# A fixed convolution moved from VectorE to TensorE: one more chunk of channels as Toeplitz products

## The chip, the cores and the metric

The kernel runs on one core of one Trainium2 chip. A core has five engines that run their own instruction streams: TensorE (PE: matrix products into PSUM), VectorE (DVE), ScalarE (ACT), GpSimd (POOL) and SyncE (SP, which here only issues DMA). The metric is the device time of one execution in microseconds, the median over several runs.

## What is computed

A Perceiver-like network of four layers with 1024 tokens (16 batches of 64) of 256 features; each layer has a cross-attention, a mixer and a feed-forward part. All is float32. The change concerns the mixer of layer 1, a Mamba-like block with a fixed, not input-dependent, state space. Cut to what matters:

```python
xz = rmsnorm(x) * norm_w @ in_proj_w.T + in_proj_b
x_ssm, gate = split(xz, 2)                                # 512 channels each
xc = conv_general_dilated(x_ssm, conv_w, ...)             # dense over channels, 4 taps in time
x_ssm = silu(xc + conv_b)
A_bar = exp(sigmoid(dt) * A)
K = einsum('dn,dn,dnl->dl', C_param, B_bar, A_bar ** l_range)   # 64 taps for each channel
ssm = causal_depthwise_conv(x_ssm, K) + x_ssm * D_param   # "the fixed convolution"
out = (ssm * silu(gate)) @ out_proj_w.T + out_proj_b
```

The fixed convolution gives each of 512 channels its own causal filter of 64 taps over the 64 tokens of a batch.

## The kernel before

The twelve blocks of the network follow one another in one program (`BLOCKS`). The mixer is `mamba_conv`. Inside it, and inside the attention before it (`xattn_folded("L1_xattn")`), `set_order(True)` makes PE, DVE and ACT each run their instructions in the order in which the Python code issues them (`mm` and `tr`, L207 and L210, for PE; the `Queue` objects `dve` and `act`, L72, for the others). So almost all instructions of this stage carry the line of a helper: L208 products, L211 transposes, L72 all of DVE and ACT; the names of their tiles tell them apart. SP's and POOL's DMA queues are put in order by the scheduler, and run first in, first out.

The 512 channels lie in four chunks (c = 0 to 3) of 128 partitions, the 1024 tokens along the free axis in two halves (n = 0, 1) of 512.

- `project(i, n)` (L1236): two products of 512 columns into `psi`; i = 0 to 3 gives the input `xp` of chunk i (ACT adds the bias), i = 4 to 7 the gate `gs` of chunk i - 4 (ACT's silu). It is a generator that can be stopped after its first product.
- `convolved(c, n)` (L1261): the dense four-tap convolution, 16 products of 512 columns into `psc`, then ACT's silu into `xs`. A generator too, stopping after every four products.
- The fixed convolution is done in two ways. For chunks 0, 1 and 2 `taps` (L1278) lets DVE do the 64 taps, each a multiply and add of the shifted tokens by a per-channel scalar, into two accumulators (even and odd taps) that are summed at the end; `gated` (L1291) multiplies by the gate into `o`. For chunk 3 it is a Toeplitz product on PE: `tokens` (L1294) transposes `xs[3]` so that tokens lie on partitions (`xt`), `toeplitz(i, ...)` (L1303) takes 32 channels at a time; for each channel d it multiplies that channel's 64 x 64 Toeplitz matrix with the channel's tokens, twice (for partitions 0 to 63 and 64 to 127), 8 columns each (`psT`), and ACT copies the block into `yt`. At the end `pso` transposes it back and DVE gates it into `o`.
- `part(c, t)` (L1320): the output projection of chunk c for token tile t, one product of 256 columns accumulated in PSUM (`po`) over the chunks; `added` adds it to the residual `X`.

The Toeplitz matrices are made in the attention before: `conv_taps` (L1152) computes the filters and writes those of chunk 3, with zeros ahead, to DRAM (`d_K`, L1190); then `tap_rows(s)` (L1193), called four times at each of 16 steps of the attention's loop (L867 to L869), copies one shifted window of it, DRAM to DRAM, into row s of `d_T` (L1195), 32 KB. These 64 copies go out on SP's queue, among the attention's loads of `cT` (L657, L659) and `cx` (L666). In `toeplitz` SP loads the matrices of 32 channels into `T` (L1307), two DMAs of 512 KB, four buffers.

The order of the stage: projections and convolution of chunk 0, gate of chunk 0, DVE starts chunk 0's taps; PE goes on with the convolutions of chunks 1, 2 and 3, while DVE does the taps of 1 and 2; then `tokens`, and `toeplitz` with other work dealt into it: before every sixth channel (`every`) it takes one step of the generator `rest` (L1326), that is the gates 5, 6, 7, then `part` of chunk 0, the gating of chunk 1 on DVE, and `part` of chunk 1. What is left of `rest` follows, then `gated` and `part` of chunk 2, then the transposes, gating and `part` of chunk 3 with the residual sums.

## Time and profile before

| | |
|---|---|
| median of 3 runs | 3028.03 us (3027.95 to 3032.76) |
| the profiled execution | 3034.92 us, span 3033.2 us |
| PE / DVE / ACT / POOL busy | 95% / 64% / 44% / 24% |
| mean granted clock of PE | 0.965 |
| the mixer `mamba_conv`, from its first projection to its last `po` | 1153 to 1344 us |
| DVE's taps of chunks 0, 1, 2 | 1177.0 to 1316.1 us |
| row copies `d_T<-d_K` on SP | 64, from 895.2 to 944.1 us, 2.3 us from issue to landing |
| loads `T<-d_T` on SP | 8, issued 1177.0 to 1181.4 us, 6.9 us to landing |

The profile is one execution. Times on the left of a timeline's line count from the span's start; the bracket gives how long the engine was idle before the group and what ended that. PE counts as busy while any product is in flight, so a busy PE can still be a slow one: the column PEclk gives the share of its full clock that the chip's throttle granted. Each product of this float32 kernel stands in the profile as two records. The granted clock is 1.00 in most of the span, and 0.50 in stretches.

### The profile page before, as it was taken

The page shows a single profiled execution, that of the slowest core. Times are in us where ns is not written, and L with a number is a line of the kernel's source. Part 1 is how long each engine was busy: PE and PEld are TensorE (multiplying, and loading weights), DVE is VectorE, ACT ScalarE, POOL GpSimd, SP SyncE. Part 2 cuts the span into 40 slices and gives each one's busy share as a digit, 9 for nine tenths or more (in the row PEclk, how much of TensorE's full clock was granted, in tenths as well). Part 3 has the DMA queues.
Part 4 walks back from the last instruction along what each step waited for, and adds up shares of the span by engine and source line. Part 5 has one row for each costly group of instructions (what it writes and reads, how often), then busy time and mean ns, then how long its engine had stood idle before and what let it go on. Part 6 is the DMA issues. An engine that isn't in the chain of part 4 may idle for free.

```text
span 3033.2 us, 65778 instructions
## 1 busy us (share of the span) xinstructions
PE 2872.8 (95%) x27656; PEld 1824.3 (60%) x27656; DVE 1951.5 (64%) x4061; ACT 1322.6 (44%) x3049; POOL 737.7 (24%) x817
## 2 busy tenths in 40 slices
PE   8999999999999999987999999997999899998889
PEld 4666666666555554466875555546985454545677
DVE  6888886524776665952127777768975667775521
ACT  4555554412554441002335444448951255554222
POOL 1000002400210001014530100026961454542142
PEclk9999999999999999978999999998999999999889
DMA  2011000014223313026862222201111211110243
GB/s 75 23 44 33 23 30 13 18 35 113 65 82 96 102 47 85 21 70 244 294 237 64 75 75 80 61 22 39 57 54 40 67 59 63 66 46 15 73 141 124
DMA packets 75839, 225.26 MB, mean 74 GB/s; under 512 B 17431, under 2 KB 30586, under 8 KB 68632
## 3 DMA queue, kind: packets, MB, share of 16 engines
q1 hardware_dynamic: 47568, 115.57, 12.6%
q0 software_dynamic: 21728, 99.34, 9.7%
q10 hardware_dynamic: 6248, 6.14, 0.7%
q8 instruction: 219, 3.59, 0.5%
q14 instruction: 76, 0.62, 0.1%
HBM read 210.09 MB, written 14.49 MB: 74 GB/s over the span
## 4 chain that ended last, share of the span: by engine, by line
PE 80%; DVE 13%; ACT 2%; POOL 2%; issue 2%; DMA 1%; DVEq 0%; POOLq 0%; ACTq 0%; SPq 0%
PE pss L208 15%; PE o L208 14%; PE pu L208 8%; PE pd L208 7%; PE psp L208 6%; PE pkv L208 6%; PE pst L211 4%; PE po L208 2%; PE psq L208 2%; PE pb L208 2%; DVE h L72 1%; PE psy L208 1%; PE py L1655 1%; PE pg L208 1%; PE ptk L211 1%
## 5 line engine op out<-in xcount | busy, mean ns | idle before, releaser
L208 PE MATMUL pss<-cT,qw 128*32 128x256 f32 x8192 | 360.8, 381 | 5.7 <-ACT pr L72 5.7
L72 DVE TENSOR_REDUCE nm<-pss 128x2 f32<-128x512 f32 (+1 forms) x384 | 314.5, 861 | 68.6 <-PE pss L208 68.5
L208 PE MATMUL o<-pT,cx 128*64 128x512 f32 (+3 forms) x1088 | 351.7, 576 | 0.0
L72 ACT ACTIVATE pr<-pss,nmm 128x256 f32<-128x256 f32 x512 | 234.4, 484 | 151.1 <-DVE nmm L72 151.1
L208 PEld LDWEIGHTS pss<-cT,qw 128*32 128x32 f32 x8192 | 201.1, 108 | 133.0 <-issue 18.2
L225 POOL TENSOR_SCALAR rs<-mv 128x8 f32<-128x8 f32 (+3 forms) x50 | 10.0, 200 | 1084.1 <-DVE mv L243 609.6
L208 PEld LDWEIGHTS o<-pT,cx 128*64 128x64 f32 (+1 forms) x1088 | 134.3, 163 | 188.4 <-issue 167.1
L208 PE MATMUL pkv<-wx,cT 128*128 128x512 f32 (+1 forms) x512 | 193.4, 632 | 0.6 <-issue 0.6
L72 ACT ACTIVATE pr<-pr,sm 128x256 f32<-128x256 f32 x256 | 109.1, 497 | 192.5 <-DVE sm L72 192.5
L72 DVE TENSOR_SCALAR pr<-pr,sm 128x256 f32<-128x256 f32 (+1 forms) x384 | 169.6, 484 | 6.3
L211 PEld LDWEIGHTS pst<-ident,pr 128*128 128x128 f32 x1024 | 114.5, 141 | 69.1 <-DVE pr L72 25.0
L208 PE MATMUL pd<-wd,hT 128*128 128x256 f32 x656 | 151.6, 382 | 2.6 <-DVE hT L2903 1.4
L72 DVE STREAM_TRANSPOSE pT<-pr 128x1024 f32<-128x1024 f32 x128 | 151.8, 1224 | 2.2
L2661 DVE TENSOR_SCALAR y<-pd,row 128x256 f32<-128x256 f32 x39 | 18.9, 484 | 205.3 <-PE pd L208 205.3
L1648 POOL TENSOR_TENSOR h<-h,cb 128x1024 f32<-128x1024 f32 x63 | 147.2, 2390 | 11.5 <-DVE h L72 11.3
L72 DVE TENSOR_TENSOR_SCAN h<-dA,pb 128x512 f32<-128x512 f32 x128 | 145.3, 1200 | 4.8 <-PE pb L211 2.2
L72 ACT ACTIVATE pr<-pss,nm 128x1024 f32<-128x1024 f32 x128 | 141.9, 1117 | 3.0 <-DVE nm L72 3.0
L208 PEld LDWEIGHTS pd<-wd,hT 128*128 128x128 f32 x656 | 122.1, 190 | 30.3 <-DVE hT L2903 5.6
L211 PE MATMUL pst<-ident,pr 128*128 128x128 f32 x1024 | 136.0, 276 | 2.0 <-DVE pr L72 1.3
L208 PEld LDWEIGHTS pkv<-wx,cT 128*128 128x128 f32 (+1 forms) x512 | 64.5, 189 | 118.3 <-issue 92.2
L1881 POOL TENSOR_TENSOR rnk<-rnk,mhalf 128x8 f32<-128x8 f32 (+1 forms) x84 | 130.0, 1548 | 7.0
L72 ACT COPY pT<-pst 128x512 f32<-128x512 f32 x128 | 75.0, 586 | 127.5 <-PE pst L211 127.5
(567 smaller groups left out, 5820.4 us busy)
## 6 DMA issues: line engine op xcount, KB each, us to landing
cT<-in_ctxT SPq DMA_DIRECT2D x32, 768.0 KB, 4.3
cx<-in_ctxP SPq DMA_DIRECT2D x32, 768.0 KB, 4.2
cT<-in_ctxT SPq DMA_DIRECT2D x32, 512.0 KB, 3.9
cT<-in_ctxT SPq DMA_DIRECT2D x64, 256.0 KB, 4.9
offb<-d_off SPq DMA_DIRECT2D x16, 576.0 KB
cb<-d_C SPq DMA_DIRECT2D x16, 512.0 KB, 3.7
wu<-in_L_ffn_w POOLq DMA_DIRECT2D x8, 1024.0 KB, 5.5
wd<-in_L_ffn_w POOLq DMA_DIRECT2D x8, 1024.0 KB, 6.2
```

Of the source, the lines that this page charges most:

```text
L72: ins = getattr(self.engine, op)(*args, **kwargs)
L208: self.in_order(self.nc.tensor.matmul(out, lhsT=lhsT, rhs=rhs, start=start, stop=stop))
L211: self.in_order(self.nc.tensor.transpose(out, in_, self.ident))
L225: nc.gpsimd.tensor_scalar(t[:p, :n], in_, scale, eps, ALU.mult, ALU.add)
L1648: nc.gpsimd.tensor_tensor(hs[i], hs[i], cbs[hf, g], ALU.mult)
L1655: nc.tensor.matmul(py[:, t, ch], lhsT=x, rhs=self.ident, start=start, stop=stop, is_transpose=True, skip_group_check=True,)
L1881: nc.gpsimd.tensor_tensor(r, r, self.mhalf[:, : n * H], ALU.pow)
L2661: nc.vector.tensor_scalar(y[:, i, :], po[:, i * D : (i + 1) * D], weight[:, g + i : g + i + 1], None, ALU.mult)
```

## The change

The fixed convolution of chunk 2 goes the way of chunk 3, as Toeplitz products on PE; DVE keeps the taps of chunks 0 and 1. For this
- two sets of filters are written (`d_K[0]`, `d_K[1]`), and every `tap_rows` issues two copies, 128 in all;
- the order becomes: convolutions of chunks 1 and 3, taps of chunk 1, `tokens(3)`, `toeplitz(3)` with the convolution of chunk 2 dealt in (one step of four products before every 14th channel), `tokens(2)`, `toeplitz(2)` with `rest` dealt in (before every fifth channel);
- `rest` now has the gates 7, 5, 6; after gate 7 the transposes back and the gating of chunk 3 (`channels(3)`), after gate 5 the gating of chunk 1; then `part` of chunks 0, 1 and 3. `channels(2)` and `part` of chunk 2 end the stage;
- 16 loads of `T` instead of 8 through the same four buffers.

```diff
-        self.d_K = dram.tile([P, 2 * TQ - 1], F32, name="d_K")
-        self.d_T = dram.tile([TQ, P, TQ], F32, name="d_T")
+        self.d_K = [dram.tile([P, 2 * TQ - 1], F32, name=f"d_K{c}") for c in (2, 3)]
+        self.d_T = [dram.tile([TQ, P, TQ], F32, name=f"d_T{c}") for c in (2, 3)]
...
-        zk = pool.tile([P, 2 * TQ - 1], F32, name="tapz")
+        zk = pool.tile([P, 2, 2 * TQ - 1], F32, name="tapz")
         nc.gpsimd.memset(zk, 0.0)
-        nc.gpsimd.tensor_copy(zk[:, TQ - 1 :], self.taps[:, 3, :])
-        nc.sync.dma_start(out=self.d_K, in_=zk)
+        nc.gpsimd.tensor_copy(zk[:, :, TQ - 1 :], self.taps[:, 2:4, :])
+        for i in range(2):
+            nc.sync.dma_start(out=self.d_K[i], in_=zk[:, i])
...
-        self.nc.sync.dma_start(out=self.d_T[s], in_=self.d_K[:, TQ - 1 - s : 2 * TQ - 1 - s])
+        for i in range(2):
+            self.nc.sync.dma_start(out=self.d_T[i][s], in_=self.d_K[i][:, TQ - 1 - s : 2 * TQ - 1 - s])
...
-            def tokens(g):
+            def tokens(c):
...
-            def toeplitz(i, more, every):
+            def toeplitz(c, i, more, every):
                 T = two.tile([P, TB, TQ], F32, tag="T", name="T", bufs=4)
...
                 for d in range(TB):
                     if (i * TB + d) % every == 0:
                         next(more, None)
                     for r in (slice(0, 64), slice(64, 128)):
-                        self.mm(ps[r, d, :], T[r, d, :], xt[r, :, i * TB + d])
+                        self.mm(ps[r, d, :], T[r, d, :], xts[c][r, :, i * TB + d])
...
+            def channels(c):
+                for g in range(2):
+                    ps = mid.tile([P, 512], F32, tag="m", name="pso")
+                    for k in range(4):
+                        self.tr(ps[:, k * P : (k + 1) * P], yts[c][:, 4 * g + k, :])
+                    cols = slice(g * 512, (g + 1) * 512)
+                    dve.tensor_tensor(o[:, c, cols], ps, gs[:, c, cols], ALU.mult)
...
             def rest():
-                for i in (5, 6, 7):
+                for i in (7, 5, 6):
                     for h in range(2):
                         yield from project(i, h)
-                for t in range(0, NT, 2):
-                    part(0, t)
-                    part(0, t + 1)
-                    yield
-                gated(*sums[1])
-                for t in range(0, NT, 2):
-                    part(1, t)
-                    part(1, t + 1)
-                    yield
+                    if i == 7:
+                        channels(3)
+                    if i == 5:
+                        gated(*last_sum)
+                for c in (0, 1, 3):
+                    for t in range(0, NT, 2):
+                        part(c, t)
+                        part(c, t + 1)
+                        yield
...
-            for c in (1, 2, 3):
+            for c in (1, 3):
                 for n in range(2):
                     conv(c, n)
-                if c < 3:
-                    sums[c] = taps(c, 0, B)
-            for g in range(2):
-                tokens(g)
+            last_sum = taps(1, 0, B)
+            tokens(3)
+            more = (x for n in range(2) for x in convolved(2, n))
+            for i in range(P // TB):
+                toeplitz(3, i, more, 14)
+            for _ in more:
+                pass
+            tokens(2)
             more = rest()
             for i in range(P // TB):
-                toeplitz(i, more, 6)
+                toeplitz(2, i, more, 5)
             for _ in more:
                 pass
-            gated(*sums[2])
-            for t in range(NT):
-                part(2, t)
...
+            channels(2)
...
             for t in range(NT):
-                part(3, t)
+                part(2, t)
```

More of the change, by code (lines that the diff above doesn't have):

```diff
@@ L1228, in mamba_conv @@
             gs = one.tile([P, 4, N], F32, name="gs")
-            xt = one.tile([P, NT, P], F32, name="xt")
-            yt = one.tile([P, NT, P], F32, name="yt")
+            xts, yts = ({c: one.tile([P, NT, P], F32, name=f"{n}{c}") for c in (2, 3)} for n in ("xt", "yt"))
             o = one.tile([P, 4, N], F32, name="o")
@@ L1292, in gated @@
                 dve.tensor_tensor(o[:, c, cols], acc.rearrange("p b t -> p (b t)"), gs[:, c, cols], ALU.mult)
-            def tokens(g):
-                ps = mid.tile([P, 512], F32, tag="m", name="pst")
-                x = xs[3].rearrange("p b t -> p (b t)")
-                for k in range(4):
-                    t = 4 * g + k
-                    self.tr(ps[:, k * P : (k + 1) * P], x[:, t * P : (t + 1) * P])
-                act.copy(xt[:, 4 * g : 4 * g + 4, :], ps.rearrange("p (t d) -> p t d", t=4))
-            def toeplitz(i, more, every):
+            def tokens(c):
+                x = xs[c].rearrange("p b t -> p (b t)")
+                for g in range(2):
+                    ps = mid.tile([P, 512], F32, tag="m", name="pst")
+                    for k in range(4):
+                        t = 4 * g + k
+                        self.tr(ps[:, k * P : (k + 1) * P], x[:, t * P : (t + 1) * P])
+                    act.copy(xts[c][:, 4 * g : 4 * g + 4, :], ps.rearrange("p (t d) -> p t d", t=4))
+            def toeplitz(c, i, more, every):
                 T = two.tile([P, TB, TQ], F32, tag="T", name="T", bufs=4)
                 for r in range(2):
-                    ins = nc.sync.dma_start(out=T[64 * r : 64 * r + 64], in_=self.d_T[:, i * TB : (i + 1) * TB, :])
+                    ins = nc.sync.dma_start(
+                        out=T[64 * r : 64 * r + 64], in_=self.d_T[c - 2][:, i * TB : (i + 1) * TB, :]
+                    )
                     tc.add_manual_dep(ins.ins, started[0], sync, reason="behind the taps' weights")
@@ L1313, in toeplitz @@
                     for r in (slice(0, 64), slice(64, 128)):
-                        self.mm(ps[r, d, :], T[r, d, :], xt[r, :, i * TB + d])
-                act.copy(yt[:, :, i * TB : (i + 1) * TB], ps.rearrange("p d t -> p t d"))
+                        self.mm(ps[r, d, :], T[r, d, :], xts[c][r, :, i * TB + d])
+                act.copy(yts[c][:, :, i * TB : (i + 1) * TB], ps.rearrange("p d t -> p t d"))
+            def channels(c):
+                for g in range(2):
+                    ps = mid.tile([P, 512], F32, tag="m", name="pso")
+                    for k in range(4):
+                        self.tr(ps[:, k * P : (k + 1) * P], yts[c][:, 4 * g + k, :])
+                    cols = slice(g * 512, (g + 1) * 512)
+                    dve.tensor_tensor(o[:, c, cols], ps, gs[:, c, cols], ALU.mult)
             pos = [held.tile([P, 2, D], F32, tag="o", name="po") for _ in range(NT // 2)]
             def part(c, t):
-                first, last = t % 2 == 0 and c == 0, t % 2 == 1 and c == 3
+                first, last = t % 2 == 0 and c == 0, t % 2 == 1 and c == 2
                 self.mm(pos[t // 2][:, t % 2], o[:, c, t * P : (t + 1) * P], wo[:, c, :], first, last)
-            sums = {}
             def rest():
-                for i in (5, 6, 7):
+                for i in (7, 5, 6):
                     for h in range(2):
                         yield from project(i, h)
-                for t in range(0, NT, 2):
-                    part(0, t)
-                    part(0, t + 1)
-                    yield
-                gated(*sums[1])
-                for t in range(0, NT, 2):
-                    part(1, t)
-                    part(1, t + 1)
-                    yield
+                    if i == 7:
[7 more added lines that the diff above has]
+                        yield
             for c in range(4):
@@ L1349, in mamba_conv @@
                 gated(*x)
-            for c in (1, 2, 3):
+            for c in (1, 3):
                 for n in range(2):
                     conv(c, n)
-                if c < 3:
-                    sums[c] = taps(c, 0, B)
-            for g in range(2):
-                tokens(g)
+            last_sum = taps(1, 0, B)
[6 more added lines that the diff above has]
+            tokens(2)
             more = rest()
             for i in range(P // TB):
-                toeplitz(i, more, 6)
+                toeplitz(2, i, more, 5)
             for _ in more:
                 pass
-            gated(*sums[2])
-            for t in range(NT):
-                part(2, t)
-            for g in range(2):
-                ps = mid.tile([P, 512], F32, tag="m", name="pso")
-                for k in range(4):
-                    self.tr(ps[:, k * P : (k + 1) * P], yt[:, 4 * g + k, :])
-                cols = slice(g * 512, (g + 1) * 512)
-                dve.tensor_tensor(o[:, 3, cols], ps, gs[:, 3, cols], ALU.mult)
+            channels(2)
             def added(lo, hi):
```

## The prediction, made before the changed kernel ran

> **What bounds the kernel now.** I read the page first, then the chain of waits, then the timelines of PE, DVE and SP, and last the granted clock by stretches of 3.41 us.

> ```profile
> span 3033.2 us, 65778 instructions
> PE 2872.8 (95%) x27656; PEld 1824.3 (60%) x27656; DVE 1951.5 (64%) x4061; ACT 1322.6 (44%) x3049; POOL 737.7 (24%) x817
> ```

> PE is busy 95% of the span, so work added to it costs time unless it fills a hole. The profiled execution took 3034.92 us (span 3033.2); the median of the runs is 3028.03, 6.9 lower. Durations below are the profile's, and the difference is put on the median.

> The change lies between 1177 and 1345 us. From 1177.02 to 1317.4 the chain of waits runs over DVE's taps. Chunk 2's taps run from 1272.98 to 1316.13:

> ```profile
> 1272.98 0.75 DVE L72 TENSOR_SCALAR acc20e<-xs,taps 128x1024 f32<-128x1024 f32 x1
> ...
> 1317.27 1.22 DVE L72 TENSOR_TENSOR o<-acc20e,gs 128x1024 f32<-128x1024 f32 x1
> ```

> PE's timeline there (start, length, idle time before it in brackets):

> ```profile
> 1198.43 82.61 PE L208 MATMUL psc<-xp,wc 128*128 128x512 f32 x192
> ...
> 1301.80 0.87 PE L208 MATMUL psT<-xt,T 64*64 64x8 f32 x24
> 1302.60 1.12 PE L208 MATMUL psi<-xnT,w_in 128*128 128x512 f32 x2
> ...
> 1311.09 0.87 PE L208 MATMUL psT<-xt,T 64*64 64x8 f32 x24
> 1317.40 2.08 PE L208 MATMUL po<-wo,o 128*128 128x256 f32 x4 [5.44 <-DVE o L72]
> 1319.41 1.45 PE L208 MATMUL psT<-xt,T 64*64 64x8 f32 x24
> 1320.79 2.07 PE L208 MATMUL po<-wo,o 128*128 128x256 f32 x4
> ...
> 1329.57 3.16 PE L208 MATMUL psT<-xt,T 64*64 64x8 f32 x56
> 1332.66 6.08 PE L208 MATMUL po<-wo,o 128*128 128x256 f32 x16
> 1338.57 1.04 PE L211 MATMUL pso<-ident,yt 128*128 128x128 f32 x8
> 1340.02 3.72 PE L208 MATMUL po<-wo,o 128*128 128x256 f32 x16 [0.42 <-DVE o L72]
> ```

> PE works without a hole until 1311.96, waits 5.44 us for DVE, and is then slow: the same 24 small records take 1.45 us for 0.87, four `po` records 2.07 for 1.13. The granted clock says why (columns: stretch, its length, PE busy, PEld, DVE, ACT, POOL, PEclk, DMA, GB/s):

> ```profile
> 1306.74:1310.16 3.42, 3.42 (x57) 2.64 (x56) 3.42 (x9) 0.00 (x0) 0.00 (x0) 1.00 0.22 87
> 1310.16:1313.57 3.41, 1.80 (x28) 1.32 (x28) 3.41 (x12) 0.37 (x1) 0.00 (x0) 1.00 0.00 0
> 1313.57:1316.98 3.41, 0.00 (x0) 0.00 (x0) 3.38 (x10) 0.00 (x0) 0.00 (x0) 0.50 0.00 0
> ...
> 1323.81:1327.22 3.41, 3.41 (x34) 2.56 (x34) 0.00 (x0) 0.00 (x0) 0.00 (x0) 0.50 0.00 0
> ...
> 1334.05:1337.46 3.41, 3.41 (x9) 2.70 (x8) 0.00 (x0) 0.00 (x0) 0.00 (x0) 0.50 0.00 0
> 1337.46:1340.88 3.42, 3.00 (x18) 2.48 (x17) 1.29 (x2) 0.00 (x0) 0.00 (x0) 1.00 0.00 0
> ```

> **What PE gets, and what it saves.** A product shows as two records. Unit prices at full clock: 512 columns 0.4294 us (82.44/192, from 1198.43 to 1280.87), 256 columns half of it, a transpose 0.133 (1.04/8). Of 24 small records the starts span 0.87-0.20 = 0.67 us, 29 ns a record, 0.117 us for a channel's four. A round of 24 small and two wide records takes 1.85 us; less 0.70 and 0.86 this leaves 0.285 us for changing to small products and back.

> From 1198.43 the new order on PE is:
> - four half chunks of convolution (chunks 1 and 3), 128 x 0.4294 = 54.96: 1253.39;
> - tokens(3), as now from 1280.87 to 1282.31, 1.44: 1254.83;
> - toeplitz(3) with chunk 2's convolution dealt in: 64 x 0.4294 + 128 x 0.117 + 8 rounds x 0.285 = 27.48 + 14.95 + 2.28 = 44.71: 1299.54;
> - tokens(2), eight transposes and a handover, 1.2: 1300.7;
> - toeplitz(2): 14.95 + 24 rounds x 0.285 (6.84) + 24 `psi` records (10.31) + 48 `po` records (10.31) + eight transposes of channels(3) (1.06) = 43.47: 1344.2;
> - the last `yt` copy, today behind 16 `po`, now bare: 0.37 and two handovers, 0.7: 1344.9.

> There the closing transposes (`pso`) start, today at 1338.57: **+6.3 us**. Put otherwise, PE gets 21.3 us (14.95 small, 12 more rounds 3.4, 16 transposes and a handover 2.3, the bare copy 0.7) and gets back 15.0: the 5.44 us wait and some 9.5 us of half clock. For the order of now the same sum at full clock and without the wait ends at 1323.6; with both put in it ends at 1338.5, against 1338.57.

> Removed from DVE: chunk 2's 64 taps, their sum and gate, 44.3 us. It is worth only those 15.0, because PE comes next, directly. Added to DVE: two 128x512 gates (0.69 each, free since 1274). Added to ACT: two `xt` copies (0.58) and four `yt` copies (0.37), beside PE; ACT is 44% busy. Uncovered, these would cost 4 us.

> **SP's queue.** 64 more row copies (`tap_rows`, L1195) and eight more loads of T (0.6 us issue, landing 6.9). The first T of chunk 2 can issue when block 0 of chunk 3 is done (near 1267) and is used after 1301: hidden; uncovered it would cost 7 us. The queue behind them holds nothing until the next stage's write. The row copies stand among the attention's loads:

> ```profile
> 938.31 6.36 SPq L1195 DMA_DIRECT2D d_T<-d_K  x10
> 948.50 0.33 SPq L657 DMA_DIRECT2D cT<-in_ctxT  x1
> 978.90 3.66 PE L208 MATMUL pss<-cT,qw 128*32 128x256 f32 x64
> ```

> Up to 938.3 the queue has as many rows ahead of each load as now. Then 35 rows, a `cx`, 17 rows, and the cT now issued at 948.50. At 0.65 to 0.77 us a row (the groups x10 to x31) it issues at 972 to 979, lands 4.9 later, at 977 to 984, and scores start at 978.90: 0 to 5 us, I take 1.5 (0.70 a row). The `cx` behind 22 more rows lands near 997, used at 999.94: hidden. The two 127-column writes and doubled copy on POOL: nothing, the rows wait for the first write as now.

> **The clock.** The last wide product of chunk 2 goes in at channel 98. Then 30 channels (3.5 us of small products) and eight transposes run without one. To weigh this I counted, for every 3.41 us window, the share in which columns stream (0.84 ns a column and record: 0.4294/512; overlaps once). All 23 windows after which the clock fell have at most 0.42, the 798 after which it stayed at least 0.42; it rose after 24 of at least 0.82, and stayed half after 46, all but one at most 0.71. Small products alone stream 0.23, transposes 0.80, the dealt rounds 0.5 to 0.57: these neither lose the clock nor win it back. A window inside the small stretch loses it: 0.23 x 3.5 + 0.8 x 1.06 over 4.6 us is 0.36. Afterwards two places can win it back, tokens(2) with its wide product and channels(3) with its; what happens depends on where the window begins. Working the sum through all places:
> - 53%: the clock holds or is back after one window. With the tail (13 small channels, bare copy, transposes: usually half clock for the last 16 `po`, some 1.5 us after what DVE's sums hide) +7 to +10.
> - 30%: half clock until channels(3). Four rounds of 3.18 for 1.73 (20 x 0.0535 + 0.40 + 1.71) and 16 slow transposes: +14 to +18.
> - 17%: half clock through toeplitz(2): 24 x 1.45 = 35, transposes and rest 3: +43 to +47.

> [...]

> **Sum:** +6.3, tail 1.5, SP 1.5, and 1.7 for one window at half clock in part of the places: +11, **3039 us** (3046 in a profile like this one). The likeliest case's own range, +7 to +10 and SP's 0 to 5, is 3035 to 3043.

> **The rivals.**
> - Half clock until channels(3): +14 to +18 and SP's 1.5, 3046. For it: nothing rose below 0.82 but pure wide or transposing windows. Against: only a third of the places.
> - Half clock through all of toeplitz(2): 45 and SP's 1.5, 3074. For it: 1320 to 1334 above. Against: it needs an unlucky place in most runs.
> - Faster: the small products run in the shadow of the wide ones they are dealt among, and DVE's 44 us are the whole story. The place is toeplitz; it decides when a channel costs PE less than about 0.068 us instead of 0.117, for then the 21.3 falls under 15.0 (128 x 0.049 = 6.3). Hidden fully, 3028 - 15.0 + 6.4 for rounds, transposes and copy = 3019. Against it: the round at 1301.80 takes 1.85 us where two wide records alone take 0.86.
> - No difference: the parts cancel (rounds cheaper when wide products come eight at a time, the clock kept): 3028 to 3034.

> **How the numbers follow.** Forecast 0.48, half clock to channels(3) 0.25, long half clock 0.15 (the median needs more than one such run), no difference 0.07, faster 0.05. The range 3031 to 3055 leaves out the faster and the long case, 0.20; its top takes SP's 5 on the second case. 0.2% (6 us) is about what can be told from no change: faster 0.04, same 0.11, slower 0.85.

> **What would show it.** DVE's taps end near 1274 and no PE wait for DVE `o` of 5 us remains; `psT` records double; `pso` of chunk 2 starts 6 us later at full clock, and the rows of 3.41 us after 1296 show whether PEclk is 0.50 and until when; the 978.90 `pss` starts 0 to 5 us later. Wrong, if `psT` groups beside convolutions run at much under 29 ns a record, if the closing transposes start before 1338, or if the attention stage lengthens by over 5 us.

## The result, and the profile after

The changed kernel takes 3040.7 us (median; 3031.82 to 3073.41), the kernel before beside it 3027.99: a ratio of 1.0046, 95% interval 1.0027 to 1.0064, so 8 to 19 us slower. Its runs lie in three groups: ten at 3031.8 to 3038.1, nine at 3039.9 to 3043.5, three at 3066.0 to 3073.4. The first two are only 1.8 us apart, and together they spread over 11.6 us, hardly more than the kernel before (3025.38 to 3035.45, 10.1 us); what is new are the three runs far above. The mean granted clock is 0.970 to 0.974 in the low group, 0.969 to 0.970 in the middle one, 0.959 to 0.960 in the high one.

The head of the page of the profiled execution (3041.78 us, so one of the middle group):

```profile
span 3040.1 us, 66858 instructions
PE 2883.5 (95%) x28184; PEld 1830.9 (60%) x28184; DVE 1908.1 (63%) x3997; ACT 1326.6 (44%) x3055; POOL 738.5 (24%) x817
```

DVE is busy 43.4 us less, PE 10.7 us more. PE's timeline of the changed stage, to set beside the one of before:

```profile
1292.51 3.70 PE L208 MATMUL psc<-xp,wc 128*128 128x512 f32 x8
1296.14 3.67 PE L208 MATMUL psT<-xt,T 64*64 64x8 f32 x120
1299.74 1.47 PE L211 MATMUL pst<-ident,xs 128*128 128x128 f32 x8
1301.01 1.92 PE L208 MATMUL psi<-xnT,w_in 128*128 128x512 f32 x2
1302.85 1.13 PE L208 MATMUL psT<-xt,T 64*64 64x8 f32 x20
1303.91 1.12 PE L208 MATMUL psi<-xnT,w_in 128*128 128x512 f32 x2
...
1344.09 1.69 PE L208 MATMUL psT<-xt,T 64*64 64x8 f32 x52
1346.24 1.09 PE L211 MATMUL pso<-ident,yt 128*128 128x128 f32 x8 [0.47 <-ACT yt L72]
1347.75 5.41 PE L208 MATMUL po<-wo,o 128*128 128x256 f32 x16 [0.41 <-DVE o L72]
```

The wait of 5.44 us is gone and no hole of PE in the stage is longer than 0.5 us, yet the closing transposes (`pso`) start at 1346.24, 7.7 us later than before. The lone stretch of small records (x120) lasts 3.67 us: 29 ns a record in pitch, as when dealt. The two wide records behind the transposes take 1.92 us, those after them 1.12. The clock by stretches of 3.41 us, on the grid on which all its changes in this trace lie; such a stretch is called a window below (the columns are those of the prediction, the granted clock PEclk is the third number from the right):

```profile
1296.89:1300.31 3.42, 3.42 (x106) 3.40 (x104) 0.00 (x0) 0.42 (x2) 0.38 (x1) 1.00 1.00 207
1300.31:1303.72 3.41, 3.41 (x23) 1.91 (x23) 0.00 (x0) 1.17 (x2) 0.00 (x0) 0.50 1.01 249
1303.72:1307.13 3.41, 3.41 (x46) 1.85 (x46) 0.00 (x0) 0.69 (x1) 0.00 (x0) 1.00 0.66 144
...
1348.10:1351.52 3.42, 3.42 (x10) 2.70 (x9) 1.49 (x4) 0.00 (x0) 0.00 (x0) 0.50 0.00 0
```

PE is busy in every one of the first three. The first, nearly all small products, is followed by half clock; the second, transposes and wide products, by full clock again. The last holds most of the final 16 `po`, which take 5.41 us for 3.72. So the whole stage, up to the normalisation `xn` with which the next block begins, ends 9.4 us later; before, then after:

```profile
1348.66 2.02 DVE L252 TENSOR_SCALAR xn<-X,mv,rstd 128x256 f32<-128x256 f32 x6 [1.49 <-POOL rstd L226]
```

```profile
1358.09 2.03 DVE L252 TENSOR_SCALAR xn<-X,mv,rstd 128x256 f32<-128x256 f32 x6 [1.49 <-POOL rstd L226]
```

DVE, whose taps end at 1273.3, has only gates left:

```profile
1309.89 1.29 DVE L72 TENSOR_TENSOR o<-pso,gs 128x512 f32<-128x512 f32 x2 [36.60 <-PE pso L211]
```

It waits 36.6 us for PE: the time taken off DVE has become waiting for PE.

### The profile page after: what moved, and what is told of

It reads as the page before. It is cut to its first block, busy times and chain, and to the rows that moved or that the text cites. A ratio compares the mean times of both kernels' runs of the same rounds, so it can differ in the third digit from the quotient of the medians.

```text
span 3040.1 us, 66858 instructions
## 1 busy us (share of the span) xinstructions
PE 2883.5 (95%) x28184; PEld 1830.9 (60%) x28184; DVE 1908.1 (63%) x3997; ACT 1326.6 (44%) x3055; POOL 738.5 (24%) x817
## 4 chain that ended last, share of the span: by engine, by line
PE 84%; DVE 9%; ACT 2%; POOL 2%; issue 2%; DMA 1%; DVEq 0%; POOLq 0%; ACTq 0%; SPq 0%
PE pss L208 14%; PE o L208 13%; PE pu L208 8%; PE pd L208 7%; PE psp L208 6%; PE pkv L208 5%; PE pst L211 4%; PE psc L208 4%; PE po L208 2%; PE psq L208 2%; PE pb L208 2%; DVE h L72 1%; PE psi L208 1%; PE psy L208 1%; PE py L1661 1%
## 5 line engine op out<-in xcount | busy, mean ns | idle before, releaser
L208 PE MATMUL pss<-cT,qw 128*32 128x256 f32 x8192 | 360.8, 381 | 5.7 <-ACT pr L72 5.7
L72 DVE TENSOR_REDUCE nm<-pss 128x2 f32<-128x512 f32 (+1 forms) x384 | 314.4, 860 | 69.1 <-PE pss L208 68.9
L208 PE MATMUL o<-pT,cx 128*64 128x512 f32 (+3 forms) x1088 | 351.7, 576 | 0.0
L72 ACT ACTIVATE pr<-pss,nmm 128x256 f32<-128x256 f32 x512 | 234.8, 485 | 151.6 <-DVE nmm L72 146.2
L208 PEld LDWEIGHTS pss<-cT,qw 128*32 128x32 f32 x8192 | 200.6, 108 | 133.1 <-issue 17.9
L225 POOL TENSOR_SCALAR rs<-mv 128x8 f32<-128x8 f32 (+3 forms) x50 | 10.1, 201 | 1084.5 <-DVE mv L243 609.1
L208 PEld LDWEIGHTS o<-pT,cx 128*64 128x64 f32 (+1 forms) x1088 | 134.3, 163 | 188.3 <-issue 167.1
L208 PE MATMUL pkv<-wx,cT 128*128 128x512 f32 (+1 forms) x512 | 193.2, 631 | 0.6 <-issue 0.6
L72 ACT ACTIVATE pr<-pr,sm 128x256 f32<-128x256 f32 x256 | 109.1, 497 | 191.6 <-DVE sm L72 191.6
L72 DVE TENSOR_SCALAR pr<-pr,sm 128x256 f32<-128x256 f32 (+1 forms) x384 | 169.3, 483 | 6.3
L211 PEld LDWEIGHTS pst<-ident,pr 128*128 128x128 f32 x1024 | 114.4, 141 | 69.2 <-DVE pr L72 25.0
L208 PE MATMUL pd<-wd,hT 128*128 128x256 f32 x656 | 151.6, 382 | 2.6 <-DVE hT L2909 1.4
L72 DVE STREAM_TRANSPOSE pT<-pr 128x1024 f32<-128x1024 f32 x128 | 151.8, 1224 | 2.2
L1654 POOL TENSOR_TENSOR h<-h,cb 128x1024 f32<-128x1024 f32 x63 | 147.3, 2385 | 11.6 <-DVE h L72 11.3
L72 DVE TENSOR_TENSOR_SCAN h<-dA,pb 128x512 f32<-128x512 f32 x128 | 145.3, 1200 | 4.9 <-PE pb L211 2.1
L72 ACT ACTIVATE pr<-pss,nm 128x1024 f32<-128x1024 f32 x128 | 142.0, 1118 | 2.8 <-DVE nm L72 2.7
L208 PEld LDWEIGHTS pd<-wd,hT 128*128 128x128 f32 x656 | 122.1, 190 | 30.3 <-DVE hT L2909 5.6
L211 PE MATMUL pst<-ident,pr 128*128 128x128 f32 x1024 | 136.0, 276 | 2.0 <-DVE pr L72 1.3
L208 PEld LDWEIGHTS pkv<-wx,cT 128*128 128x128 f32 (+1 forms) x512 | 64.5, 189 | 118.4 <-issue 92.5
L72 ACT COPY pT<-pst 128x512 f32<-128x512 f32 x128 | 75.1, 587 | 127.4 <-PE pst L211 127.4
```

The lines of the kernel that those rows point to most:

```text
L72: ins = getattr(self.engine, op)(*args, **kwargs)
L208: self.in_order(self.nc.tensor.matmul(out, lhsT=lhsT, rhs=rhs, start=start, stop=stop))
L211: self.in_order(self.nc.tensor.transpose(out, in_, self.ident))
L225: nc.gpsimd.tensor_scalar(t[:p, :n], in_, scale, eps, ALU.mult, ALU.add)
L1654: nc.gpsimd.tensor_tensor(hs[i], hs[i], cbs[hf, g], ALU.mult)
```

## The experiments

Differences are against the kernel before on the same chip; the interval of the ratio is given in us of its median (3028 to 3033).

**Dealing that reaches the end of chunk 3** (`deal18`)

```diff
-                toeplitz(3, i, more, 14)
+                toeplitz(3, i, more, 18)
```

> The changed kernel, but chunk 2's wide products are dealt one half block every 18 channels' worth of small products instead of 14, so that they reach channel 126 of chunk 3 instead of 98; the work is the same. Theory A (the clock follows the share of streamed columns in stretches of 3.41 us; the lone small products of channels 99 to 127 lose it): with no lone stretch left, no run stands above +10 us against the kernel before, the middle run at +7.0 (3035), the clock full until the closing transposes, which start at 1344.6. Theory B (the clock falls only where PE stands idle): the runs spread as those of the changed kernel, 3032 to 3073 with a middle of 3041, since PE's idle times are the same. Theory C (the changed kernel's scatter has nothing to do with this stretch): as B, and half clock elsewhere.

3043.77 against 3029.57, +14 us (interval +9 to +19); all six runs between 3038.66 and 3047.91. A fails in its numbers: the middle is 7 us above its +7, five of the six runs stand above its +10, and the closing transposes start at 1347.89 and not at 1344.6, because the clock is not full until then. The middle would fit B and C. That no run is above 3066 says little by itself: a kernel with three such runs in 22 would show none in six some four times in ten. B falls by the trace, for the clock falls while PE is busy all the time. PE, then the clock:

```profile
1268.34 2.27 PE L208 MATMUL psT<-xt,T 64*64 64x8 f32 x72
1270.54 5.40 PE L208 MATMUL psc<-xp,wc 128*128 128x512 f32 x8
```

```profile
1267.49:1270.90 3.41, 3.41 (x76) 2.56 (x75) 3.38 (x13) 0.00 (x0) 0.00 (x0) 1.00 0.77 166
1270.90:1274.32 3.42, 3.42 (x5) 1.33 (x4) 0.49 (x1) 0.00 (x0) 0.00 (x0) 0.50 0.00 0
```

Of the seven pieces of 72 small records (18 channels, 2.27 us) in this trace, three are followed by a window at 0.50, in which the eight wide records take 5.40 us for the 3.70 of full clock (from 1270.54, 1283.89 and 1297.25), 5.1 us in all. Counted as in the prediction, columns streamed in 0.44, 0.44 and 0.47 of the three windows that hold those pieces, above the 0.42 that the prediction had as the most after which the clock fell. This share alone does not tell when: counted the same way in the trace of the changed kernel, the clock fell after a window with 0.43 (from 2044.41) and held after one with 0.40 (from 2249.21).

**Dealing that ends early** (`deal8`)

```diff
-                toeplitz(3, i, more, 14)
+                toeplitz(3, i, more, 8)
```

> The changed kernel, but chunk 2's wide products are dealt every 8 channels, so that they are used up by channel 56 and the last 71 channels of chunk 3 are small products alone, 8.3 us; the work is the same. Theory A (share of streamed columns): such a stretch always holds a whole stretch of 3.41 us, so the clock falls in every run. The low group of the changed kernel's runs (+4 to +10) goes: fastest at +11, middle at +15.5 (3043), one run in five near +50. Theory B (only idle time lowers the clock): PE is as busy as in the changed kernel, so 3032 to 3073 with a middle of 3041, and the clock at 1.00 through the small stretch.

3075.78 against 3029.57, +41 us (+33 to +49): one run at 3054.19, five at 3073.28 to 3082.05. No run is in the low group, as A says, and the clock falls behind a window in which PE was busy for all of its 3.41 us, which B excludes. But the middle that A expected is missed by 33 us, and where A has one run in five near +50 there are five of six: full clock came back in far fewer runs than I counted. PE, then the clock:

```profile
1290.88 9.51 PE L208 MATMUL psT<-xt,T 64*64 64x8 f32 x254
1302.01 2.08 PE L208 MATMUL psT<-xt,T 64*64 64x8 f32 x34 [1.62 <-issue]
1304.02 1.97 PE L211 MATMUL pst<-ident,xs 128*128 128x128 f32 x8
1305.78 1.92 PE L208 MATMUL psi<-xnT,w_in 128*128 128x512 f32 x2
```

```profile
1292.69:1296.10 3.41, 3.41 (x124) 3.41 (x122) 0.00 (x0) 0.34 (x1) 0.00 (x0) 1.00 0.89 262
1296.10:1299.51 3.41, 3.41 (x72) 3.41 (x68) 0.00 (x0) 0.03 (x1) 0.00 (x0) 0.50 1.00 216
...
1302.93:1306.36 3.43, 3.43 (x29) 3.17 (x29) 0.00 (x0) 1.29 (x3) 0.00 (x0) 0.50 0.62 127
1306.36:1309.77 3.41, 3.41 (x23) 1.64 (x22) 0.00 (x0) 0.25 (x1) 0.00 (x0) 0.50 1.05 240
```

The clock falls at 1296.10. The next stretch without small records, the eight transposes and the two wide records, is 3.6 us long at half clock (1304.02 to 1307.62), only 0.2 us longer than a window. Here the grid cuts it at 1306.36, each of the two windows holds a part of it only, and the clock is 0.50 in both. The groups of 20 small records behind it take 1.24 us each up to the last at 1379.04, where the changed kernel has 0.75, and `pso` of chunk 2 starts at 1385.63.

**A longer piece to win the clock back** (`back8`: the edit above, and)

```diff
             more = rest()
+            for _ in range(4):
+                next(more)
             for i in range(P // TB):
```

> The kernel with chunk 2's wide products dealt every 8 channels (measured at +46 in the middle, five runs of six at +44 to +52), and one gate's four wide products (both halves) put in one piece behind the transposes of chunk 2, ahead of its small products, instead of being dealt among them; the work is the same. Theory A (a clock once lost comes back only behind a stretch of 3.41 us that is nearly all wide products or transposes; at half clock the eight transposes and the piece last 8.8 us and always hold one): the long half clock goes, no run above +20, middle +13 (3043). Theory B (the clock is lost for good in this stage once it is lost, or comes back after a time): as without the piece, middle +45.

3044.52 against 3033.45, +12 us (+8 to +16), all five runs at 3039.21 to 3048.24: A, with its number. The same clock loss, the same work, and some 29 us less by where eight wide records stand. B is excluded. PE, then the clock:

```profile
1303.47 1.97 PE L211 MATMUL pst<-ident,xs 128*128 128x128 f32 x8
1305.23 5.64 PE L208 MATMUL psi<-xnT,w_in 128*128 128x512 f32 x8
...
1312.54 0.75 PE L208 MATMUL psT<-xt,T 64*64 64x8 f32 x20
```

```profile
1305.95:1309.37 3.42, 3.42 (x5) 1.33 (x4) 0.00 (x0) 0.59 (x2) 0.00 (x0) 0.50 1.01 225
1309.37:1312.78 3.41, 3.41 (x22) 1.83 (x22) 1.29 (x2) 0.89 (x2) 0.00 (x0) 1.00 0.02 2
```

The eight records of `psi` fill the window from 1305.95 to 1309.37, the clock is full from there, and the first 20 small records (0.75 us) are fast. In `deal8` they took 1.24.

**Finer dealing to the end** (`fine8`)

```diff
-                    if i % 4 == 3 and i < 15:
+                    if i % 2 == 1 and i < 15:
                         yield
...
-                toeplitz(3, i, more, 14)
+                toeplitz(3, i, more, 8)
```

> The changed kernel with chunk 2's wide products dealt in pieces of four records every 8 channels instead of eight records every 14: the last piece goes in at channel 120, no small stretch is longer than 1.2 us before the closing ones, and there are 8 rounds more. Theory A (falls of the clock at a share of streamed columns below some 0.45, price of a round 0.285 us): the sum of the order is +6.3 and 8 x 0.285 = 2.3, the clock full until the tail, closing transposes near 1347, +8.5 to +10.5 in every run, middle +9.5 (3039), no run near +15 or +45. Theory B (the scatter of the changed kernel comes from elsewhere): three groups at +7, +15 and +45 as with the changed kernel. Theory C (finer dealing is free, rounds cost nothing): +6 to +7.

3044.04 against 3033.45, +10.6 us (+6 to +15), and all five runs within 3.6 us of one another (3040.90 to 3044.50): A. The clock over the 41 us of `toeplitz(2)`, and PE's end of them:

```profile
1303.58:1344.50 40.92, 40.92 (x538) 27.13 (x537) 2.51 (x3) 5.99 (x11) 0.70 (x1) 1.00 0.20 52
```

```profile
1347.45 1.56 PE L211 MATMUL pso<-ident,yt 128*128 128x128 f32 x8 [0.47 <-ACT yt L72]
```

The first dealt wide record starts at 1255.52, `pso` 91.93 us later, all at full clock. In the changed kernel it is 1255.06 to 1346.24, 91.18, of which one window at half clock is 1.7: 89.5. So eight rounds more cost 2.4 us, 0.31 each. This kernel has nothing wrong with its clock ahead of the tail and is still slower than the kernel before: the order itself is the cost.

**DVE's taps left out of the kernel before** (`cut`, and `cut2` with 2 in place of 40)

```diff
-            def taps(c, lo, hi):
+            def taps(c, lo, hi, n=TQ):
...
-                for l in range(2, TQ):
+                for l in range(2, n):
...
-                    sums[c] = taps(c, 0, B)
+                    sums[c] = taps(c, 0, B, TQ if c < 2 else 40)
```

> The kernel before, but chunk 2's taps 40 to 63 are left out on DVE (24 of 64 taps of a quarter of the tokens are not added), so that DVE is done with chunk 2 some 16 us earlier and PE has no reason to wait. It measures what the wait for DVE really costs the kernel before. Theory A (the wait of 5.44 us also halves the clock for what follows, 9.5 us more): -14.8 us (3013), closing transposes at 1323.5. Theory B (only the wait itself counts, the slow rounds after it have another reason): -5.4 us (3022.6), closing transposes at 1333. Theory C (DVE's work returns as a wait elsewhere): 0.

> The kernel before with only the first two of chunk 2's 64 taps on DVE (62 taps of a quarter of the tokens are left out), so that DVE is free of them some 43 us earlier than in the kernel before, 27 us earlier than with 24 taps left out (which gave -12 us). Theory A (behind DVE's sum PE's own order is the bound, so chunk 2's 44 us on DVE are worth only the wait and the half clock): no more than with 24 taps left out, -11.5 to -15 us (3015 to 3018), closing transposes at 1323.5 to 1326. Theory B (DVE's time itself counts, as the change's removal of it seems to say): each 10 us more off DVE shorten the kernel further, to some -40 us.

3017.59 against 3029.57, -12 us (-16 to -7), and 3017.74 against 3033.45, -16 us (-20 to -12). Both contain -14.8 and exclude -5.4; the 27 us more that `cut2` takes off DVE bring nothing that can be told, and -40 is excluded. `pso` starts at 1325.81 and 1325.16, 2.3 and 1.7 us later than A's 1323.5: in both the 16 `po` behind the last 56 small records take 5.41 us for 3.72, as they do in the changed kernel with one window at 0.50. In `cut2` DVE waits for PE, as in the changed kernel:

```profile
1325.87 1.29 DVE L72 TENSOR_TENSOR o<-pso,gs 128x512 f32<-128x512 f32 x2 [27.92 <-PE pso L211]
```

So the whole gain to be had from DVE's chunk 2 was 12 to 16 us, without any cost on PE.

**SP's part alone** (`rows`)

```diff
-        self.nc.sync.dma_start(out=self.d_T[s], in_=self.d_K[:, TQ - 1 - s : 2 * TQ - 1 - s])
+        for d in (self.d_T, self.d_U):
+            self.nc.sync.dma_start(out=d[s], in_=self.d_K[:, TQ - 1 - s : 2 * TQ - 1 - s])
```

> The kernel before with each of the 64 row copies (tap_rows) issued twice, the second into a matrix that nothing reads: the change's part on SP's queue alone. Theory A (the trace of the changed kernel: attention's scores start no later, SP's queue has slack): 0 (-1 to +1). The prediction's step: the loads behind the rows are late by 0 to 5 us, taken as +1.5. Theory C (the added writes of 4 MB disturb the attention's loads): +3 or more.

Ratio 1.0001, interval 0.9990 to 1.0011, +0.3 us (-3 to +3): nothing. The scores (`pss`) that start at 978.90 in the kernel before start at 979.32, 0.42 later, but so does the group ahead of them (977.42 against 977.00), and they wait for nothing.

**The other way round: let PE reach chunk 1's products earlier** (`early`)

```diff
-                for i in (5, 6, 7):
+                for i in (6, 7):
...
-                gated(*sums[1])
...
-                if c < 3:
+                if c == 1:
+                    projects(5, 0, 1)
+                    gated(*taps(1, 0, B))
+                if c == 2:
                     sums[c] = taps(c, 0, B)
...
-                toeplitz(i, more, 6)
+                toeplitz(i, more, 7)
```

> The kernel before, but gate 5 is projected right behind chunk 1's convolution and chunk 1's sum is gated on DVE before chunk 2's taps, so that PE can start chunk 1's output products without the later gate; two wide gate projections move ahead and one half of a gate's products is dealt every 7 small channels instead of 6. DVE's work in sum and its end for chunk 2 are the same. Theory A (PE wants cover of wide products during DVE's last taps, and gets it if its own order is right): the wait ends with DVE's sum at 1318 as before, but less of PE's work is left behind it and the clock is full: -14.3 us (3013.7; from -16 to -12.5), closing transposes near 1324. Theory B (DVE's 140 us of taps are the bound of the stage): 0, the wait moves to another place and the clock falls again.

3014.48 against 3029.57, ratio 0.9944 (0.9927 to 0.9960), -17 us (-22 to -12): A. It is faster than both kernels, with the same work as the kernel before. In that kernel PE could not deal chunk 1's `po` among the last small products, because their gating stood behind chunk 2's taps on DVE. Here it stands ahead of them; PE, and then DVE:

```profile
1318.77 2.85 PE L208 MATMUL psT<-xt,T 64*64 64x8 f32 x92
1321.57 3.72 PE L208 MATMUL po<-wo,o 128*128 128x256 f32 x16
```

```profile
1320.29 1.23 DVE L72 TENSOR_TENSOR o<-acc20e,gs 128x1024 f32<-128x1024 f32 x1
```

DVE's last gating ends at 1321.52 and PE takes it at 1321.57, without a wait and at full clock; `pso` follows at 1325.12. Both engines now end together. The last 92 small records stand together for 2.85 us, longer than the 72 of `deal18`, and the clock holds here: the grid cuts the piece at 1319.40, and columns stream in 0.54 and 0.47 of the two windows that share it. Whether it holds in the other five runs is not shown.

**A shorter order on PE in `early`** (`early16`)

```diff
                     if (i * TB + d) % every == 0:
                         next(more, None)
+                        next(more, None)
...
-                toeplitz(i, more, 7)
+                toeplitz(i, more, 16)
```

> The kernel with gate 5 and chunk 1's gating moved ahead (measured at -17 by the ratio, -15 by the medians), with the wide work dealt in pieces twice as long every 16 channels instead of every 7: eight rounds of 0.285 us fewer, so that PE's order ends 2.3 us sooner. In the trace without this edit chunk 2's gated sum lands on DVE at 1321.52 and PE takes it at 1321.57. Theory A (DVE's taps and PE's order now end together, so a shorter order on PE only waits): no gain, PE waits some 2 us for DVE o before the first po of chunk 2, -14 (from -17 to -11) against the kernel before. Theory B (PE's order alone is still the bound): 2.3 us more, -17 to -19.

3021.34 against 3033.08, -10 us by the ratio (-14 to -7), -12 by the medians: no gain, as A says.

```profile
1318.76 5.41 PE L208 MATMUL po<-wo,o 128*128 128x256 f32 x16 [2.30 <-DVE o L72]
```

PE waits 2.30 us for DVE, and the window behind the wait (1320.04 to 1323.46) is at 0.50: the 16 `po` take 1.7 us more. Against `early` the difference of some 3 to 7 us is not settled: the intervals overlap. B, which has -17 to -19, is outside the interval.

## Why the prediction was right, point by point

- *The order on PE, +6.3.* Right. From the first dealt wide record to `pso` the prediction has 90.1 us (1254.83 to 1344.9), the trace 91.18 with one window at half clock, 89.5 without. `fine8` has 91.93 where the same sum plus eight rounds gives 92.3. The unit prices held: 29 ns a small record dealt or not, 0.31 for a round where 0.285 was taken.
- *DVE's 44 us are worth only 15.* Right, by `cut` and `cut2` together, -12 and -16, and no more that can be told with 27 us more taken away. The 5.4 us of the wait alone are excluded: the half clock behind the wait counts too. Taking the wait away is what counts; `early` does it at no price on PE.
- *SP's queue, 1.5.* This term was mis-sized: it is 0. The cT that I expected to issue at 972 to 979 issued at 973.95, and PE's scores started at 979.14 against 978.90, an offset that the trace had before. `rows` bounds it at -3 to +3.
- *The tail, 1.5.* Right: from `pso` to DVE's first `xn` 11.85 us (1346.24 to 1358.09) against 10.09 (1338.57 to 1348.66), because one window at half clock takes in the last 16 `po`.
- *The sum.* +11 was said and +12.7 measured, 8 to 19. Without SP's term the sum is 9.5, and the stage of the trace is 9.4 us longer up to the first `xn`. The other 3 us of the median lie inside the interval and their cause is open, so that 3039 came within 2 us of 3040.7 is in part luck. For a profiled execution the same sum gave 3046, and 3041.78 came: besides SP's term, the stages behind the first `xn`, which the change does not touch, took 1682.0 us there against 1684.6 before.
- *The clock.* Right in kind. In `deal18` and `deal8` it fell to 0.50 behind windows in which PE was busy for all 3.41 us with 72 and 124 small records, and in `back8` it was 1.00 again behind a window full of wide records (1305.95 to 1309.37). The sizes were off. The clock fell behind a share of 0.47, where the prediction had 0.42 at the most (`deal18`). It rose behind less than 0.82 too: the window from 1300.31 in the changed kernel streams in 0.75 of its time and was followed by full clock, that from 1302.54 in `back8` streams in 0.75 too and was not. In the traces of the kernel before and of the changed one full clock followed on 48 of the 49 windows at half clock that stream in 0.73 or more, and not on one with 0.92 (before, from 2050.85); what decides there is open. In `deal8`, where the transposes and wide records behind the fall last 3.6 us, five of six runs lie in the long case, where one in five was expected.
- *The three cases.* They were given 53, 30 and 17 in 100; of 22 runs 10, 9 and 3 lie in the three groups, 45, 41 and 14 in 100. This likeness is no evidence for the shares. The profiled run is in the middle group, and its trace is the first case: one window at half clock, then full clock until the tail. The untouched stages behind the first `xn` take 1676.1 us (`early`) to 1684.7 (`early16`) in the traces, a spread wider than the 5.9 us between the medians of the low and the middle group, so these two groups need not differ in the changed stage at all. The high group does bear the mark of the third case: its mean clock of 0.959 to 0.960 is near that of the five long runs of `deal8`, 0.956 to 0.958. No trace of such a run of the changed kernel was taken.
- *The rivals.* Half clock to `channels(3)` is seen in no trace of the changed kernel, and the one trace of a run near its 3046 does not have it. Half clock through `toeplitz(2)` is, by the mean clocks, what the three high runs have; three of 22 do not make the median. The faster rival falls by the pitch of the small records: 120 of them undealt take 3.67 us, the pitch that they have when dealt, so nothing of them was in the shadow of wide ones. No difference falls by the interval.

## What to carry to other kernels

Before work is moved off a busy engine, sum up the order of the engine that comes next at full speed: what can be won is the wait between the two and, here, the half clock behind it, 12 to 16 us of the 44, and the moved work must cost less than that on the new engine. Look first whether a reorder takes the wait away: one gate and its gating moved ahead of taps that they did not need brought 17 us. Where products of few columns are dealt among wide ones, read the granted clock behind each piece. Here it was 0.50 behind three of the seven pieces of 72 records (`deal18`), and behind the pieces of 32 the groups of four wide records took 1.98 to 1.99 us, all alike (`fine8`). Where the clock has fallen, try one longer piece of wide work: behind the 7.3 us of transposes and wide records in `back8` (1303.47 to 1310.72) it was 1.00, behind the 3.6 us in `deal8` it was 0.50.

## What the runs showed that was not expected

- In `deal8` and `back8` PE stands idle for 1.62 and 1.87 us in the middle of 288 small records with no other work between them, after 254 records each time, with no releaser in the trace. It shows in none of the traces with shorter pieces of small products (up to 132 records). Its cause is open; it comes after the clock has fallen and does not explain the fall.
- The place of eight wide records decides over some 29 us (`deal8` against `back8`), without a change in work or data.
